# Last mixture by expert regions in DRAM, layer 0's head sums all on PE, other landing costs and another stage order

## The chip, the cores and the metric

The kernel runs as one program on one core of a Trainium2 chip. Its time is the device time of one execution in microseconds. Six resources matter here: PE (TensorE, matmuls and transposes), DVE (VectorE), ACT (ScalarE), POOL (GpSimd), SP (SyncE, which only issues transfers) and the 16 DMA engines that carry all transfers, whichever engine issued them. Each engine executes its own instructions strictly in program order. An instruction that waits for a semaphore holds up everything behind it on that engine, and nothing on the others.

## The reference, cut to what matters

Input `x` is 16 batches of 256 tokens of 128 numbers, and there is a context of 64 keys per batch. Four layers follow one another, and each has an attention to the context and a feed-forward part, added to `x` with a gate.

```python
x = x + tanh(g_xattn[0]) * L0_attention(layernorm(x), ctx)   # softmax over the 16 heads
x = x + tanh(g_ffn[0])   * L0_ffn(layernorm(x))              # 8 experts, top 2, and a shared expert
x = x + tanh(g_xattn[1]) * L1_attention(layernorm(x), ctx, bias, mask)
x = x + tanh(g_ffn[1])   * L1_ffn(layernorm(x))              # ternary weight
x = x + tanh(g_xattn[2]) * L2_attention(layernorm(x), ctx, mask)
x = x + tanh(g_ffn[2])   * L2_ffn(layernorm(x))              # one expert in effect
x = x + tanh(g_xattn[3]) * L3_attention(layernorm(x), ctx, masks)
x = x + tanh(g_ffn[3])   * L3_ffn(layernorm(x))              # 8 experts, the best one
```

Two parts are touched. In layer 0 the attention's softmax runs over the heads, not over the keys:

```python
energy = einsum('bhqd,bhkd->bhqk', Qh, Kh) * scale
attn = softmax(energy, axis=1)                   # axis 1 is the 16 heads
out = einsum('bhqk,bhkd->bhqd', attn, Vh)
```

The last feed-forward part sends each token to the one expert with the largest probability:

```python
logits = t @ switch_w + switch_b
route_prob = softmax(logits, axis=-1)
route_prob_max = max(route_prob, axis=-1)
routes = argmax(route_prob, axis=-1)
for e in range(8):
    y = gelu(t @ w1[e] + b1[e]) @ w2[e] + b2[e]
    out = where((routes == e)[:, None], y, out)
out = out * route_prob_max[:, None]
```

## The kernel before

All of `x` stays in SBUF, one tile `xs[b]` per batch. The work is written as some hundreds of generators ("tasks"): for example `unit0(pair, t)` is layer 0's attention for two batches and half of their queries, `attention(l, b)` is that of one batch in layers 1 to 3, and `sorted_pair(l, hf, q)` is two expert tiles. The batches form two halves, `hf` 0 and 1, of eight batches or 2048 tokens, and every mixture of experts works by half. Two batches form a block (`blk`).

**What sets the order.** A planner, the class `Order`, runs the tasks when the program is built. Each task states its next step as an engine, an estimated length and the things it needs, or as a transfer with a size, or as a buffer that it wants. The planner always takes the step that can begin first by its own estimate, and among equals the one of the lowest rank (`RANKS`, one number per half and stage; stages 0 and 1 are layer 0's attention and mixture, 7 is the last mixture). Its order is then the written order of each engine; POOL is chained in the same order. A transfer is taken to land `LAND` us after its issue plus its size over `RATE`, and an indirect gather 2.2 us after its issue. These numbers decide only the order. The chip's semaphores decide when things run.

**Layer 0's attention** (`unit0`, L816 to L927): scores on PE (L833), their largest over the heads on DVE (L844, L849), differences (L852), exponentials on ACT (L865), sums over the 16 heads, reciprocals, products on POOL (L894), values on PE (L910). The sums have two forms. For the first half, 16 matmuls with the identity add up the heads in a PSUM bank (L871), and DVE takes the reciprocal from it (L877). For the second half, POOL adds eight heads to eight (L883), and DVE adds up the rest (L886) and takes the reciprocal (L889). The buffer of L883 comes from the same four `big` buffers that hold the experts' hidden values.

**Layer 0's mixture** (`mixture` with `l` = 0): each block is normalized and its rows stored to DRAM (`keep`); when all four blocks of the half have their logits, one chain of DVE steps finds the experts and every token's place in an order sorted by expert, padded to tiles of 128 rows. A matmul with a one-hot matrix (L1528 to L1549) turns that into a list, for every row of every tile, of the token that belongs there. There are 39 tiles in each half. For every tile, SP reads the tile's expert number into a register and fetches this expert's packed weights (578 KB, L1647, six buffers), POOL gathers the tile's rows by an indirect transfer (L1671), PE transposes them (L1684) and multiplies by the first weights (L1698), ACT applies the gelu (L1705, or its tanh form in layer 3), PE multiplies by the second weights (L1717), and DVE adds the bias (L1727). The results are stored and later gathered back per token (`collect`, L1779, L1787).

**The last mixture** (`mixture` with `l` = 3) does the same with one expert per token, 23 tiles per half. Its DRAM rows hold the normalized row and `x` itself (`keep` and `keep_x`, issued by SP). The one-hot list also carries the token's gate, in three bfloat16 parts. The tile's result, times the gate, plus `x` (L1734), goes straight to its rows of the output by an indirect scatter on POOL (L1753). POOL so issues 124 gathers of rows (78 for layer 0, 46 here), 64 gathers of `collect` and 46 scatters.

Other lines that are named below: L644 and L647 to L650 belong to the layernorm (DVE, then POOL), L669 and L747 to the queries, L972 prepares layer 1's attention bias, loaded by SP four transfers a batch into one of three buffers, L1093 takes the scores' largest in layers 2 and 3, and L1392 adds the router's bias.

## Time and profile before

| | |
|---|---|
| Median of 3 runs | 1087.75 us (1085.69 to 1087.98) |
| The profiled execution, reported time | 1091.78 us |
| The profiled execution, span of its instructions | 1090.0 us |
| Granted PE clock, mean over the span | 0.927 |
| DMA bytes | 114.36 MB, 105 GB/s over the span |

| Stage in the profiled execution | from, us | to, us |
|---|---|---|
| Layer 0's attention, first half (`unit0`) | 20.6 | 110.4 |
| Layer 0's attention, second half | 106.8 | 281.5 |
| Layer 0's expert tiles, first half | 171.4 | 342.9 |
| Layer 0's expert tiles, second half | 337.1 | 516.7 |
| Layer 1's attention, both halves | 419.1 | 769.0 |
| Layer 2's attention, both halves | 551.0 | 887.1 |
| Layer 3's attention, both halves | 649.3 | 963.6 |
| Last mixture's routing, first half | 798.7 | 851.2 |
| Last mixture's expert tiles, first half | 855.6 | 1072.9 |
| Last mixture's routing, second half | 971.5 | 994.2 |
| Last mixture's expert tiles, second half | 984.2 | 1087.2 |

The second table is made from the trace: each instruction of DVE, ACT and POOL was put to its task by its place in the engine's order, and the first start and the last end of each task's instructions were taken. The end of the first half's last tiles (1072.9) is that of their scatters on POOL.

In the profile's lines, `x` and a number is a count of instructions, and "busy" is the time in which an engine executed an instruction. Matmul records overlap, as matmuls are pipelined: 16 records of L1698 in a row pass in 1.79 us though each lasts some 300 ns. A 128-wide matmul in float32 leaves two records. In a table by stretches of time, each engine's busy time is followed by its number of instructions, and then come the granted PE clock (1 is full speed), the mean busy share of the DMA engines and the bytes moved per second. In the chain of waits, each line is a start, a length and the work, and "issue" is time in which the engine waited for nothing that the profile shows. In a group's line, the busy time, the mean of one in ns, and the idle time before the group with what ended most of it stand at the right.

### The profile page before, as it was taken

The page shows a single profiled execution, that of the slowest core. Times are in us where ns is not written, and L with a number is a line of the kernel's source. Part 1 is how long each engine was busy: PE and PEld are TensorE (multiplying, and loading weights), DVE is VectorE, ACT ScalarE, POOL GpSimd, SP SyncE. Part 2 cuts the span into 40 slices and gives each one's busy share as a digit, 9 for nine tenths or more (in the row PEclk, how much of TensorE's full clock was granted, in tenths as well). Part 3 has the DMA queues.
Part 4 walks back from the last instruction along what each step waited for, and adds up shares of the span by engine and source line. Part 5 has one row for each costly group of instructions (what it writes and reads, how often), then busy time and mean ns, then how long its engine had stood idle before and what let it go on. Part 6 is the DMA issues. An engine that isn't in the chain of part 4 may idle for free.

```text
span 1090.0 us, 27621 instructions
## 1 busy us (share of the span) xinstructions
PE 914.4 (84%) x10480; PEld 724.2 (66%) x10480; DVE 670.9 (62%) x1832; ACT 575.9 (53%) x1345; POOL 644.8 (59%) x1055
## 2 busy tenths in 40 slices
PE   5887568989788987789789899999998999777765
PEld 3776346878686886677556667667665667666664
DVE  4798897754464224366776767879789645446221
ACT  5454243656443454566446557765765667553332
POOL 5787636666834654765557656533444666744675
PEclk9899788979889998899999999999999999987987
DMA  6000004467764774633100100100000425544672
GB/s 195 2 12 21 23 1 147 132 211 237 231 153 162 227 228 141 228 93 112 52 17 20 29 16 21 36 21 7 24 9 2 161 59 156 189 145 144 215 259 60
DMA packets 63477, 114.36 MB, mean 105 GB/s; under 512 B 10289, under 2 KB 42552, under 8 KB 63344
## 3 DMA queue, kind: packets, MB, share of 16 engines
q1 hardware_dynamic: 54688, 94.22, 26.8%
q0 software_dynamic: 8224, 17.45, 6.0%
q8 instruction: 82, 1.34, 0.5%
q10 hardware_dynamic: 432, 0.93, 0.3%
q14 instruction: 51, 0.42, 0.1%
HBM read 99.06 MB, written 14.42 MB: 104 GB/s over the span
## 4 chain that ended last, share of the span: by engine, by line
PE 38%; DVE 12%; issue 8%; DMA 6%; POOL 5%; ACT 3%; another core or an unknown queue 2%; SPq 0%; POOLq 0%; DVEq 0%; ACTq 0%
PE bank L1698 6%; PE bank L1717 6%; DMA xg<-xrow,state 4%; DVE mx L1093 3%; PE bank L1008 3%; PE bank L1175 3%; PE bank L1072 2%; PE bank L781 2%; PE bank L1134 2%; PE bank L1014 2%; PE bank L747 1%; PE bank L1197 1%; PE bank L669 1%; PE bank L1621 1%
## 5 line engine op out<-in xcount | busy, mean ns | idle before, releaser
L1705 ACT ACTIVATE big<-bank,wb 128x128 f32<-128x128 f32 x496 | 138.5, 382 | 156.2 <-issue 98.6
L1698 PE MATMUL bank<-xgT,wb 128*128 128x128 f32 x992 | 147.5, 301 | 21.9 <-DVE xgT L1688 14.0
L1671 POOL DMA_INDIRECT xg<-xrow,state x124 | 121.9, 983 | 63.5 <-issue 27.9
L1698 PEld LDWEIGHTS bank<-xgT,wb 128*128 128x128 f32 x992 | 134.1, 212 | 31.7 <-DVE xgT L1688 18.6
L1717 PE MATMUL bank<-wb,big 128*128 128x128 f32 x992 | 133.6, 287 | 5.8 <-issue 4.8
L1717 PEld LDWEIGHTS bank<-wb,big 128*128 128x128 f32 x992 | 126.2, 200 | 13.8 <-issue 10.9
L656 ACT ACTIVATE xn<-x,ln 128x128 f32<-128x128 f32 x256 | 107.6, 494 | 52.5 <-POOL ln L650 52.2
L1727 DVE TENSOR_TENSOR y<-bank,wb 128x128 f32<-128x128 f32 x124 | 32.3, 285 | 115.4 <-PE bank L1717 90.9
L894 POOL TENSOR_TENSOR pT<-pT,rc 128x1024 f32<-128x1024 f32 x32 | 75.2, 2366 | 45.2 <-DVE rc L889 12.3
L1779 POOL DMA_INDIRECT yg<-ysort,state x64 | 62.9, 983 | 56.5 <-DVE x L1787 26.3
L1093 DVE TENSOR_REDUCE mx<-bank 128x8 f32<-128x512 f32 x128 | 81.4, 682 | 20.9 <-PE bank L1014 6.3
L1162 ACT ACTIVATE pT<-bank 128x512 f32<-128x512 f32 x128 | 67.2, 601 | 36.3 <-PE bank L1149 30.2
L677 POOL TENSOR_TENSOR x<-x,rows_sb 128x256 f32<-128x256 f32 x96 | 71.3, 761 | 12.5 <-ACT xn L656 11.8
L644 DVE BATCH_NORM_STATS2 ln<-x 128x6 f32<-128x128 f32 x256 | 68.6, 268 | 2.4 <-DMA x<-in_x_dram 2.2
L648 POOL TENSOR_TENSOR ln<-ln,mhalf 128x4 f32<-128x4 f32 x64 | 66.7, 1043 | 5.3
L1008 PE MATMUL bank<-kexp,qT 32*128 32x256 f32 x768 | 69.4, 413 | 0.2 <-DVE mx L1093 0.2
L647 POOL TENSOR_SCALAR ln<-ln 128x4 f32<-128x4 f32 x64 | 14.7, 230 | 90.9 <-DVE ln L645 83.7
L1753 POOL DMA_INDIRECT out_dram<-y,state x46 | 47.1, 1023 | 27.6 <-DVE y L1727 20.6
L1046 DVE TENSOR_REDUCE mx<-bank 128x8 f32<-128x512 f32 x64 | 43.5, 682 | 29.8 <-PE bank L1014 14.2
L1175 PE MATMUL bank<-pT,vx 128*32 128x256 f32 x768 | 60.3, 399 | 0.8 <-DVE pT L1054 0.5
L1688 DVE COPY xgT<-bank 128x256 f32<-128x256 f32 x64 | 25.9, 409 | 55.1 <-PE bank L1684 37.9
L1684 PE MATMUL bank<-ident,xg 128*128 128x128 f32 x124 | 29.4, 306 | 34.2 <-DMA xg<-xrow,state 30.1
(230 smaller groups left out, 2094.2 us busy)
## 6 DMA issues: line engine op xcount, KB each, us to landing
wb<-in_pk_l_dram SPq DMA_DIRECT2D x124, 578.0 KB
ysort<-y SPq DMA_DIRECT2D x38, 128.0 KB
xrow<-xn SPq DMA_DIRECT2D x16, 256.0 KB
fill<-in_fsideT_dram SPq DMA_DIRECT2D x64, 64.0 KB
x<-in_x_dram SPq DMA_DIRECT2D x16, 128.0 KB
xrow<-x SPq DMA_DIRECT2D x16, 128.0 KB
xg<-xrow,state POOLq DMA_INDIRECT x124
yg<-ysort,state POOLq DMA_INDIRECT x64
```

The source lines that it names most:

```text
L644: nc.vector.bn_stats(st[:, 2 * i + j, :], xs[b][:, j, :])
L656: nc.scalar.activation(xn[:, k, :], xs[b][:, j, :], AF.Identity, bias=nm[:, k : k + 1], scale=rs[:, k : k + 1],)
L677: nc.gpsimd.tensor_tensor(xs[b], xs[b], row.unsqueeze(1).to_broadcast([P, 2, D]), ALU.add)
L894: nc.gpsimd.tensor_tensor(s3, s3, rc.ap.unsqueeze(1).to_broadcast([P, 8, P]), ALU.mult)
L1008: nc.tensor.matmul(dst(g), qT[strip(g), ts], kexp[strip(g)].rearrange("p h k -> p (h k)"), start=True, stop=False,)
L1093: nc.vector.tensor_reduce(mx[:, :, g, :], sc[g].ap.rearrange("p (t h k) -> p t h k", h=4, k=S2), AX.X, ALU.max,)
L1162: nc.scalar.activation(pTs[g // 2].ap[:, (g % 2) * 512 : (g % 2 + 1) * 512], sc[g].ap, AF.Exp)
L1175: nc.tensor.matmul(po.ap[strip(g), i * S : (i + 1) * S], vx.ap[:, b % 2, c, :], pTs[c // 4].ap[:, (c % 4) * S : (c % 4 + 1) * S], start=Tr ...
L1671: nc.gpsimd.indirect_dma_start(out=xg[i], out_offset=None, in_=xd, in_offset=bass.IndirectOffsetOnAxis(ap=index[:, 2 * q + i : 2 * q + i + ...
L1698: nc.tensor.matmul(ph.ap[:, cs], wb[i].ap[:, cs], xgT.ap[:, i * P : (i + 1) * P], start=True, stop=True,)
L1705: nc.scalar.activation(hb.ap[:, i, cs], ph.ap[:, cs], func, bias=wb[i].ap[:, PK_B1 + c : PK_B1 + c + 1],)
L1717: nc.tensor.matmul(py.ap[:, i * D : (i + 1) * D], hb.ap[:, i, c * P : (c + 1) * P], wb[i].ap[:, PK_W2 + c * D : PK_W2 + (c + 1) * D], star ...
```

## The change

Four things change.

1. **The last mixture works by expert regions.** `mixture` is split into `first_mixture` (layer 0, otherwise as before) and `last_mixture`. In DRAM every expert has a region of 2048 rows and a gap of 128, so 17280 rows per half, each of 258 numbers: the normalized row, `x`, the token's number and its gate. A running count per expert (`next_`) gives every token its row as soon as its own block's experts are known, so each block makes its own routing (30 DVE instructions in place of 9, and in place of most of the chain of 47 per half), and POOL scatters its four times 128 rows into the regions. Every tile is then 128 rows that lie one after another. SP reads the tile's first row into a register and loads them by a plain transfer. No one-hot list is made. A closing chain of 13 DVE instructions per half gives each tile's expert, first row and number of filled rows. Rows that no token fills must hold finite numbers, so `fill_regions` first writes all rows with 54 transfers of 660 kB on SP from one constant tile. Two small DVE instructions per tile give empty rows a place beyond the output, where the scatter drops them.
2. **Layer 0's sums** over the heads are made by PE in both halves.
3. **The planner's numbers:** an indirect gather of layer 0 is taken to land 3.2 us after its issue rather than 2.2, and `RATE` is 280 kB/us rather than 250.
4. **Other ranks**, so another order of the stages.

The instruction streams as built show the following. PE: of the last mixture's 46 tiles, seven are finished before the last attention matmul, where it was twelve. POOL issues 220 indirect transfers rather than 234. SP issues 382 transfers rather than 306. ACT loads its tables 26 times rather than 36.

```diff
-REACH, LAND, RATE, SWAP = 0.1, 1.8, 250e3, 1.3
+REACH, LAND, RATE, SWAP = 0.1, 1.8, 280e3, 1.3
...
-RANKS = ((11, 14, 2, 14, 3, 5, 4, 14), (14, 14, 4, 14, 6, 9, 6, 2))
+RANKS = ((0, 14, 14, 14, 1, 15, 10, 14), (14, 14, 4, 8, 9, 12, 13, 15))
...
+ROW3 = 2 * D + 2
+REGION = NT * P
+NROWS = E * REGION + (E - 1) * P
...
-        if pair < HB // 2:
-            (pb,) = yield get(banks, 1)
-            at = yield op(PE, 3.6, at, pb)
-            for h in range(H):
...
-        else:
-            (sb,) = yield get(big_s, 1)
-            sm = sb.ap.rearrange("p a b -> p (a b)")
-            at = yield op(POOL, 2.4, at, sb)
-            nc.gpsimd.tensor_tensor(sm, ss[0].ap, ss[1].ap, ALU.add)
-            (rc,) = yield get(rc0_s, 1)
-            at = yield op(DVE, 2.85, at, rc)
-            nc.vector.tensor_reduce(
-                rc.ap, sm.rearrange("p (h q) -> p q h", q=P), AX.X, ALU.add
-            )
-            nc.vector.reciprocal(rc.ap, rc.ap)
-            give(sb, big_s, at)
+        (pb,) = yield get(banks, 1)
+        at = yield op(PE, 3.6, at, pb)
+        for h in range(H):
+            nc.tensor.matmul(
+                pb.ap[:, 0:P], ident, ss[h // 8].ap[:, (h % 8) * P : (h % 8 + 1) * P],
+                start=(h == 0), stop=(h == H - 1),
+            )
+        (rc,) = yield get(rc0_s, 1)
+        at = yield op(DVE, 0.95, at, rc)
+        nc.vector.reciprocal(rc.ap, pb.ap[:, 0:P])
+        give(pb, banks, at)
...
+    def last_mixture(hf, rank, begin):
...
+        def block(blk):
...
+            (xn,) = yield get(big_s, 1, begin[bs[0]], begin[bs[1]])
+            rows = xn.ap.rearrange("p (t c) -> p t c", c=ROW3)
+            ats = yield from layernorm(blk, begin, rows[:, :, 0:D], xn)
...
+            for i, b in enumerate(bs):
+                yield op(ACT, 0.35, begin[b])
+                nc.scalar.copy(rows[:, 2 * i : 2 * i + 2, D : 2 * D], xs[b])
...
+            nc.tensor.matmul(pb.ap[:, 0:32], ones, cnt, start=True, stop=True)
+            nc.tensor.matmul(pb.ap[:, 32:64], before, cnt, start=True, stop=True)
...
+            nc.vector.tensor_copy(acc3[:, :, 0], next_)
+            nc.vector.tensor_copy(acc3[:, :, 1:5], et(pb.ap[:, 0:32]))
+            nc.vector.tensor_tensor_scan(
+                upto, carry4.rearrange("p e t -> p (e t)"), acc, 0.0, ALU.mult, ALU.add
+            )
+            nc.vector.tensor_copy(next_, upto3[:, :, 4])
...
+            for t in range(t0, t0 + 4):
+                at = yield op(POOL, 1.3, placed)
+                part_indirect()
+                ins = nc.gpsimd.indirect_dma_start(
+                    out=xd,
+                    out_offset=bass.IndirectOffsetOnAxis(ap=pos[:, t : t + 1], axis=0),
+                    in_=rows[:, t - t0, :],
+                    in_offset=None,
+                )
...
+    def fill_regions(hf, whens):
+        xd = srt[3, hf][2].rearrange("(p a) c -> p a c", p=P)
+        n, m = NROWS // P, 5
+        for i in range(n // m):
+            yield dma(SP, 4.0 * P * m * ROW3, whens[i * m * len(whens) // n])
+            nc.sync.dma_start(
+                xd[:, m * i : m * (i + 1), :],
+                rows_sb[:, 0:ROW3].unsqueeze(1).to_broadcast([P, m, ROW3]),
+            )
...
         for i in range(m):
+            if l == 3:
+                yield op(SP, 0.4, *xgs, *needs)
+                r = nc.sync.value_load(
+                    ex.ap[0:1, n + 2 * q + i : n + 2 * q + i + 1], min_val=0, max_val=NROWS - P
+                )
+                at = yield dma(SP, 132e3)
+                nc.sync.dma_start(xg[i], xd[bass.ds(r, P), :])
+                done_with(ex, at)
+                continue
             at = yield op(POOL, 1.3, *xgs, *needs)
...
-        at = (at[0] + 2.2, "DMA")
+        if l == 0:
+            at = (at[0] + 3.2, "DMA")
...
+                nc.vector.tensor_tensor(
+                    place[:, i : i + 1], xg[i][:, 2 * D : 2 * D + 1].bitcast(I32),
+                    filled[:, t : t + 1], ALU.bitwise_and,
+                )
+                nc.vector.tensor_tensor(
+                    place[:, i : i + 1], place[:, i : i + 1], empty[:, t : t + 1], ALU.bitwise_or
+                )
...
+    whens = [X[i][b] for i, h in ((5, 0), (6, 0), (3, 1), (4, 1)) for b in range(HB * h, HB * h + HB)]
+    for hf in range(2):
+        order.task(100.0, fill_regions(hf, whens[16 * hf : 16 * hf + 16]))
```

`whens` is a need of the planner alone: it says after which steps a fill may be placed, and no semaphore stands for it.

## The prediction, made before the result was known

> **What bounds the kernel now.** I first read the page's busy shares, then the same by stretches of time, then the chain of waits from the last instruction, then the groups of instructions.
>
> ```profile
> span 1090.0 us, 27621 instructions
> PE 914.4 (84%) x10480; PEld 724.2 (66%) x10480; DVE 670.9 (62%) x1832; ACT 575.9 (53%) x1345; POOL 644.8 (59%) x1055
> ...
> q1 hardware_dynamic: 54688, 94.22, 26.8%
> ```
>
> No engine fills the span, and 84% on PE is an average of unlike stretches. From the tiles' names I cut at 517 (the last layer 0 expert tile) and 964 (the last attention matmul), and subdivided.
>
> ```profile
> core 0: us, PE busy (x) PEld busy (x) DVE busy (x) ACT busy (x) POOL busy (x), PEclk, DMA share, GB/s
> 0.00:171.00 171.00, 122.00 (x1884) 95.41 (x1885) 138.70 (x313) 74.76 (x140) 108.54 (x145) 0.87 0.14 41
> 171.00:342.00 171.00, 151.84 (x1647) 129.03 (x1646) 99.13 (x245) 94.86 (x236) 106.16 (x117) 0.90 0.60 187
> 342.00:517.00 175.00, 147.93 (x1281) 128.74 (x1285) 70.86 (x205) 90.73 (x238) 105.84 (x170) 0.93 0.56 175
> 517.00:675.00 158.00, 141.15 (x1738) 98.11 (x1731) 116.72 (x329) 89.40 (x190) 94.86 (x186) 0.98 0.09 25
> 675.00:855.00 180.00, 172.01 (x2280) 123.33 (x2278) 150.30 (x440) 114.43 (x249) 83.14 (x189) 0.99 0.07 20
> 855.00:964.00 109.00, 97.40 (x1090) 73.96 (x1091) 52.65 (x161) 72.02 (x163) 69.33 (x123) 0.97 0.43 136
> 964.00:1090.00 126.00, 82.11 (x575) 75.57 (x573) 42.53 (x145) 39.73 (x134) 76.94 (x127) 0.85 0.56 177
> 1016.00:1090.00 74.00, 48.22 (x338) 44.79 (x338) 16.31 (x52) 21.06 (x76) 46.83 (x77) 0.85 0.54 169
> ```
>
> To 171 VectorE is fullest (139 of 171). From 171 to 517 PE leads and transfers are heavy. From 517 to 855 PE and VectorE are dense and transfers nearly absent. From 855 to 964 VectorE falls to half and PE from 96% to 89%: one half's layer 3 attention runs beside the other half's first expert tiles. The last 126 us finish 34 of the 46 expert tiles, 3.7 us each, with every engine idle a third of the time or more. The chain there says why:
>
> ```profile
> 984.36 11.31 issue
> ...
> 997.31 6.65 DMA xg<-xrow,state
> ...
> 1007.57 8.37 DMA xg<-xrow,state
> ...
> 1030.76 1.02 POOL out_dram L1753
> 1032.17 1.00 POOL out_dram L1753
> 1033.58 1.00 POOL out_dram L1753
> 1034.97 4.84 DMA xg<-xrow,state
> ...
> 1063.50 4.67 DMA xg<-xrow,state
> ```
>
> Gathers sit on POOL behind the result's scatters, 1.4 us apart; PE waits for them with nothing else left.
>
> **The change, part by part**, as three stretches of the profiled execution (span 1090.0, reported 1091.8; the median shown is 1087.75, so 2.2 us come off a sum of spans).
>
> ```profile
> L871 PE MATMUL bank<-pT,ident 128*128 128x128 f32 x256 | 36.0, 309 | 9.9 <-DVE pT L852 4.4 <-DVE vx L807 3.0 <-ACT pT L865 2.5
> L883 POOL TENSOR_TENSOR big<-pT,pT 128x1024 f32<-128x1024 f32 x8 | 18.9, 2360 | 20.9 <-PE bank L1607 17.9 <-ACT pT L865 3.0
> L886 DVE TENSOR_REDUCE rc<-big 128x128 f32<-128x1024 f32 x8 | 15.3, 1912 | 2.8 <-POOL big L883 2.8
> L1671 POOL DMA_INDIRECT xg<-xrow,state x124 | 121.9, 983 | 63.5 <-issue 27.9 <-PE bank L1607 27.6 <-PE bank L1717 2.9
> ```
>
> *Layer 0, to 517.* Eight units of the second half lose L883 and L886 (18.9 us of POOL, 15.3 of VectorE) and gain the first half's form: 36.0 us of PE busy, 4.5 each; the reciprocal stays. In the built order three of the eight sums stand ahead of the first routing, where PE idles 49 of 171 us: free. Five stand behind it, where PE is busy 152 of 171: 5 x 4.5 = 22.5 us added. Against that, the five no longer put 5 x 2.36 = 12 us ahead of gathers in POOL's queue (L883 once waited 17.9 us for its buffer, and everything on POOL with it), and ScalarE's table loads up to here fall from 25 to 19 in the built order, 6 x 1.28 = 8 us. I take two thirds of these 20 back: +8. Bounds: +22.5 with nothing given back, and 22.5 - 20 - 10 = -8 if VectorE's relief (5 x 1.9) counts too. The later landing (3.2 for 2.2) and the faster rate are numbers of the planner: no instruction, only order. POOL's new constants, some 2 us of memsets and iotas, fall before 60 us.
>
> *Attention, 517 to 964: 447 us.* In the built order seven expert tiles, not twelve, are finished by PE ahead of the last attention matmul, and both halves go through layers 1 to 3 closer together. So the thin part (855 to 964) should resemble the dense one. VectorE is the measure: 319.7 us busy now. Off: the first routing of layer 3 (47 instructions, 18.2), five tiles at 0.85 (4.3). On: 21 small instructions more per block, at 0.19 (L1392's 179 ns for 128x32), for six blocks 24; the closing 13 instructions 5; two per tile for seven tiles 2. That makes 328. At a VectorE share of 0.78, between the first and second dense stretch (0.74 and 0.835), 421 us: -26. Bounds: 393 at 0.835, 459 at today's whole-stretch 0.715: -54 to +12. I take the middle of the dense rows, since the work mix is theirs.
>
> Also here: 54 region fills (each 660 kB, 35.7 MB) on SP. The q1 row gives 94.22 MB in 26.8% of 1090 us, 322 GB/s, so 111 us of wire where 7 to 9% is used. They precede bias loads (L972's) by two to eight fills, at most 8 x 2.05 = 16 us of delay; those loads are issued three batches ahead, so I charge nothing. Uncovered, the four runs (2, 4, 3, 8) cost 17 x 2.05 = 35. The other 37 fills stand on SP between the last bias load and layer 3's first weight fetch, 76 us against the hundred or more that layer 2's and 3's attention of the first half still takes there. Two waits are new. A half's first region scatter waits for its 27 fills, and with it all of POOL, layernorm included; the first read of the regions waits on SP for all 16 scatters, with every later weight fetch behind it. The first is hidden by the same hundred us, the second by the six weight buffers already filled; if either cover went, the price is what is left of the 76, or one scatter's way (1.4 to issue, 4.7 to 8.4 to land in the chain's rows). The region scatters add 32 on POOL while 46 gathers leave; 24 row stores leave SP; ScalarE's 16 copies of x, 0.4 each, have slack (114 of 180 busy).
>
> *Tail: 126 us.* Of the tiles, 39 now end behind the last attention matmul. Each moves 592 + 132 + 66 = 790 kB, 2.45 us at 322 GB/s. PE needs 16 passes at 112 ns each (the chain has 16 in 1.79) and two transposes, about 2.1, or 2.5 at the clock of 0.85. SP issues two register-loaded transfers a tile, at 1.2 apart (its issues at 1009.49 and 1010.66) 2.3. POOL keeps one scatter, 1.4. VectorE 1.2. So the floor is 96 us, and the ceiling the 3.5 us a tile of 1016 to 1090 (21 tiles in 74), 137. I take 2.8, nearer the floor because the waits in the chain were for gathers that POOL issued late, and 8 us to drain: 117, so -9. Bounds -22 to +19. The second half's routing (971 to 994, a gap in PE before) now has 16 tiles of the first half to hide it.
>
> The built order puts each pair's two gathers on SP behind that pair's two weight loads; POOL had its own queue. The Trainium skill, "DMA: Bandwidth & Descriptors", Queues, rings and completion order, says each engine consumes a ring's descriptors in order, which speaks against this move: an uncovered gather would come 3.7 us later by 2 x 592 kB at 322 GB/s, 20 pairs 74 us, and the sum would be 1135. No row of before shows it, as no gather was on SP. I keep to the sum, because three pairs of buffers are in flight.
>
> Sum: 517 + 8 + 447 - 26 + 126 - 9 = 1063, less 2.2: **1061**.
>
> **Rivals.** *A, PE becomes layer 0's bound:* the five sums behind the routing cost their 22.5 and nothing comes back, +22.5 for +8: 1076. For: PE is 89% busy from 171 to 342. Against: POOL's and ScalarE's waits there.
> *B, the tail is transfer-bound at the rate it has (ends slower):* 39 x 0.79 MB at 177 GB/s is 174 us, with 8 drain 182, not 117: 1126. For: the most bytes are packed into the end. Against: single stretches of 10 us hold 329 GB/s at DMA share 0.98, so 177 is no limit of the wire. It decides at 144 us: over 3.5 a tile, under 226 GB/s.
> *C, the new order doesn't tighten the attention:* VectorE's share stays 0.715, because PE's fixed order waits on chains (layernorm, routing, bias loads) in new places: 459 for 421, 1099. For: moved priorities guarantee no density, and each block gains a serial chain of some 25 small VectorE steps. Against: 338 us at 0.79 exist already.
>
> **How the numbers follow.** Forecast 0.50 (its own range 1044 to 1074), A 0.17, B 0.13, C 0.20. 0.2% is 2.2 us, about what a measurement can tell. Faster: 0.49 + 0.15 + 0.02 + 0.04 = 0.70; same 0.04; slower 0.26, mostly B and C. The range goes from 1040 (attention and tail both halfway to their better bounds, 14 and 7 less) to 1100, just past C and short of B.
>
> **What would show it.** Right: layer 0's last expert tile near 525; last attention matmul near 946 with VectorE at 0.78 from there back; a tail of 117 us, above 250 GB/s, with no POOL scatter ahead of a gather in the chain. Wrong: PE waiting for bias loads between 525 and 750 (fills), the SP queue waiting on gathers in the tail, or tiles at over 3.5 us; or layer 0 past 540, with PE's sums on the chain.

## The result, and the profile after

| | time |
|---|---|
| before, median of 20 runs | 1090.58 us (1085.69 to 1098.28) |
| after, median of 20 runs | 1083.24 us (1072.46 to 1095.38) |
| ratio, with its 95% interval | 0.9901 (0.9878 to 0.9925) |

The change makes the kernel 1.0% faster, 7 to 11 us. The forecast was 27: the sign was right, and less than half of the size came. The kernel before took 1090 us in two of the six sets of runs below and 1036 to 1039 in the other four, for a cause that stays open, so times are compared by their ratio to the kernel before in the same set, and stages only between sets of one such level. The same cuts as in the prediction (layer 0's last expert tile, the last attention matmul, the end) give:

| stretch | before | forecast | after | difference, forecast | difference, measured |
|---|---|---|---|---|---|
| layer 0 | 517 | 525 | 526.7 | +8 | +10 |
| attention | 447 | 421 | 430.7 | -26 | -16 |
| tail | 126 | 117 | 124 | -9 | -2 |
| span | 1090.0 | 1063 | 1081.1 | -27 | -9 |

The first lines of the page of the kernel after, and its DMA queue:

```profile
span 1081.1 us, 28618 instructions
PE 932.2 (86%) x10728; PEld 745.6 (69%) x10728; DVE 675.9 (63%) x2019; ACT 569.4 (53%) x1357; POOL 610.1 (56%) x1030
...
q1 hardware_dynamic: 88160, 131.77, 42.0%
```

PE works 18 us more than before (932 for 914) in a span that is 9 us shorter, so its idle time fell by 27. VectorE, which the forecast followed, works 5 us more. The kernel after by the three stretches (the same columns as in the prediction):

```profile
0.00:171.00 171.00, 131.39 (x2016) 103.61 (x2016) 138.25 (x318) 70.23 (x135) 102.19 (x149) 0.88 0.15 43
171.00:526.70 355.70, 314.83 (x3033) 271.91 (x3032) 158.39 (x443) 184.21 (x479) 201.04 (x292) 0.94 0.57 175
526.70:957.40 430.70, 396.17 (x5030) 284.74 (x5031) 326.25 (x1010) 264.84 (x582) 247.29 (x492) 0.99 0.48 123
957.40:1081.10 123.70, 89.78 (x656) 85.37 (x654) 53.05 (x252) 50.08 (x163) 59.62 (x98) 0.86 0.69 224
```

The kernel before by the same three stretches, in rows that the prediction had only in pieces:

```profile
171.00:517.00 346.00, 299.77 (x2928) 257.77 (x2931) 169.99 (x450) 185.59 (x474) 212.00 (x286) 0.92 0.58 181
517.00:964.00 447.00, 410.56 (x5107) 295.41 (x5100) 319.66 (x928) 275.86 (x600) 247.33 (x497) 0.98 0.16 50
```

Take PE's busy time from each length. In the attention PE idled 36.4 us before (447.0 less 410.6) and idles 34.5 after (430.7 less 396.2). By this account the stretch is 16 us shorter because 14 us of PE's busy time have left it, and not because it became denser. Most of that work is not gone: five expert tiles that were finished ahead of the last attention matmul are now finished behind it. PE's transposes and multiplications of expert tiles take 32.0 us of the attention before and 20.2 after, and PE would be busy for 383.9 and 378.9 us without them: by these two counts the tiles make 9 to 12 of the 14. In the tail PE's work grew from 82.1 to 89.8 and its idle time fell from 43.9 to 33.9. To layer 0's last tile its work grew by 24.5 and its idle time fell from 95.2 to 80.5.

The chain of waits of the kernel after, at the place where the first half's tiles end and the second half's begin:

```profile
1007.88 0.30 DVE y L1899
...
1009.33 0.31 SPq L1809
...
1011.01 5.50 DMA xg<-xrow
...
1018.00 2.08 PE bank L1868 x8
...
1020.50 3.38 PE bank L1868 x16
1023.88 1.79 PE bank L1889 x16
```

L1899 is a tile's addition of the bias on VectorE, L1809 a fetch of weights on SP, `xg<-xrow` a tile's rows coming from a region, L1868 and L1889 the two multiplications (eight records a tile each). Further down, L1854 is the transposes of a tile's rows on PE, L1858 the copy of what they give (`xgT`) out of PSUM, and L1640 a matmul of the routing, which waits for VectorE's steps (`rt`). A tile's time below is the start of its L1899 in the trace. The first half's last tile is put out from 1007.9 on. The second half's first pair follows at 1014.7, and the second pair ends its multiplications at 1025.7 and is put out by 1026.9: some 19 us for four tiles, where the other 19 of the second half take 47, 2.5 each. So about 9 us are lost between the halves. The rows for that pair came at 1016.5, after a stretch in which SP, issuing in order, had been busy with weights. PE's clock in stretches of 5 us tells of a second loss there:

```profile
1010.00:1015.00 5.00, 4.79 (x29) 4.55 (x27) 0.28 (x1) 2.28 (x8) 1.23 (x3) 0.66 0.93 295
1015.00:1020.00 5.00, 2.48 (x10) 2.18 (x11) 1.81 (x9) 0.00 (x0) 2.42 (x4) 0.69 0.93 296
1020.00:1025.00 5.00, 5.00 (x31) 5.00 (x30) 0.42 (x1) 3.31 (x12) 0.00 (x0) 0.63 0.29 105
1025.00:1030.00 5.00, 4.76 (x42) 4.57 (x42) 2.02 (x9) 2.14 (x9) 2.41 (x4) 1.00 0.57 184
```

After a gap the granted clock is 0.63 to 0.69, and 16 matmuls take 3.38 us instead of 1.79. PE then counts as busy while it works at less than its pace.

The first half's last tiles, ahead of this place, are slow too: from 957.4 to 1007.9 PE finishes 16 of them in 50.5 us, 3.2 each, at a clock of 0.83, and waits 5.1 us at two strokes for the second half's routing (in the lines of waits: PE's line, what it waited for, us in total, times, longest):

```profile
957.40:1007.90 50.50, 38.57 (x267) 36.74 (x265) 28.61 (x145) 24.53 (x71) 28.86 (x48) 0.83 0.73 234
```

```profile
PE bank L1640 <- DVE rt L1320: 3.1, 1, 3.1
PE bank L1640 <- DVE rt L1319: 2.0, 1, 2.0
```

### The profile page after: what moved, and what is told of

Same layout as the page of the kernel before. It is cut to its first block, busy times and chain, and to the rows that moved or that the text cites. A ratio compares the mean times of both kernels' runs of the same rounds, so it can differ in the third digit from the quotient of the medians.

```text
span 1081.1 us, 28618 instructions
## 1 busy us (share of the span) xinstructions
PE 932.2 (86%) x10728; PEld 745.6 (69%) x10728; DVE 675.9 (63%) x2019; ACT 569.4 (53%) x1357; POOL 610.1 (56%) x1030
## 4 chain that ended last, share of the span: by engine, by line
PE 54%; DVE 23%; issue 7%; POOL 6%; DMA 4%; ACT 4%; another core or an unknown queue 1%; SPq 0%; POOLq 0%; DVEq 0%; ACTq 0%
PE bank L1868 9%; PE bank L1889 8%; PE bank L1187 4%; PE bank L1020 4%; PE bank L895 3%; PE bank L1748 2%; PE bank L1762 2%; DVE mx L1105 2%; PE bank L1146 2%; PE bank L1026 2%; PE bank L1084 2%; DVE ov L869 2%; DVE pT L877 2%; PE bank L806 2%; DVE ln L669 1%
## 5 line engine op out<-in xcount | busy, mean ns | idle before, releaser
L1868 PE MATMUL bank<-xgT,wb 128*128 128x128 f32 x992 | 140.6, 293 | 26.5 <-DVE xgT L1858 13.5
L1868 PEld LDWEIGHTS bank<-xgT,wb 128*128 128x128 f32 x992 | 129.8, 206 | 34.5 <-DVE xgT L1858 16.8
L1889 PE MATMUL bank<-wb,big 128*128 128x128 f32 x992 | 134.3, 288 | 4.3 <-ACT big L1875 2.0
L1889 PEld LDWEIGHTS bank<-wb,big 128*128 128x128 f32 x992 | 126.8, 202 | 8.9 <-ACT big L1875 4.7
L681 ACT ACTIVATE xn<-x,ln 128x128 f32<-128x128 f32 x224 | 94.0, 493 | 48.8 <-POOL ln L675 48.8
L1899 DVE TENSOR_TENSOR y<-bank,wb 128x128 f32<-128x128 f32 x124 | 32.6, 288 | 132.0 <-PE bank L1889 87.1
L1840 POOL DMA_INDIRECT xg<-xrow,state x78 | 76.0, 974 | 48.4 <-DVE state L1540 18.5
L1105 DVE TENSOR_REDUCE mx<-bank 128x8 f32<-128x512 f32 x128 | 81.0, 682 | 13.1 <-PE bank L1026 9.4
L672 POOL TENSOR_SCALAR ln<-ln 128x4 f32<-128x4 f32 x64 | 14.7, 230 | 129.3 <-DVE ln L670 121.8
L1174 ACT ACTIVATE pT<-bank 128x512 f32<-128x512 f32 x128 | 67.2, 604 | 34.0 <-PE bank L1161 30.6
L1934 POOL DMA_INDIRECT out_dram<-y x46 | 46.3, 1006 | 56.5 <-DVE y L1899 49.7
L702 POOL TENSOR_TENSOR x<-x,rows_sb 128x256 f32<-128x256 f32 x96 | 68.7, 734 | 16.0 <-ACT xn L681 15.3
L895 PE MATMUL bank<-pT,ident 128*128 128x128 f32 x512 | 69.1, 300 | 9.8 <-DVE pT L877 4.4
L895 PEld LDWEIGHTS bank<-pT,ident 128*128 128x128 f32 x512 | 67.3, 215 | 12.8 <-ACT xn L681 4.6
L1090 ACT ACTIVATE pT<-bank 128x512 f32<-128x512 f32 x64 | 37.0, 604 | 43.7 <-PE bank L1084 32.5
```

What stands on the lines that cost most here:

```text
L681: nc.scalar.activation(xn[:, k, :], xs[b][:, j, :], AF.Identity, bias=nm[:, k : k + 1], scale=rs[:, k : k + 1],)
L702: nc.gpsimd.tensor_tensor(xs[b], xs[b], row.unsqueeze(1).to_broadcast([P, 2, D]), ALU.add)
L895: nc.tensor.matmul(pb.ap[:, 0:P], ident, ss[h // 8].ap[:, (h % 8) * P : (h % 8 + 1) * P], start=(h == 0), stop=(h == H - 1),)
L1105: nc.vector.tensor_reduce(mx[:, :, g, :], sc[g].ap.rearrange("p (t h k) -> p t h k", h=4, k=S2), AX.X, ALU.max,)
L1840: nc.gpsimd.indirect_dma_start(out=xg[i], out_offset=None, in_=xd, in_offset=bass.IndirectOffsetOnAxis(ap=index[:, 2 * q + i : 2 * q + i + ...
L1868: nc.tensor.matmul(ph.ap[:, cs], wb[i].ap[:, cs], xgT.ap[:, i * P : (i + 1) * P], start=True, stop=True,)
```

## The experiments

Each is an edit of the kernel after unless it says otherwise. "Ratio" is always to the kernel before in the same set, with its 95% interval.

### The two kernels again, and the parts one by one

> The kernel before, for its stages on the same chip as the runs beside it. If PE sets the attention stretch, PE's idle time between layer 0's last expert tile and the last attention matmul is the same as in the changed kernel within 4 us (36 and 35 in the profiles at hand: 447 less 411 busy, 431 less 396). If VectorE's share sets it, the changed kernel idles less there by 10 or more.

> The changed kernel, for its stages and its ratio on the same chip as the runs beside it: 0.988 to 0.993 of the time before, layer 0 later by 5 to 12 us than in the kernel before, the attention stretch shorter by 13 to 20 and the tail by 0 to 6.

PE's idle time and the three stretches came out as expected. The ratio did not: the kernel after has 0.9947 (0.9914 to 0.9981) in this set, above the 0.988 to 0.993 that were expected. Layer 0's last tile, the last attention matmul and the end stand at 521.7, 970.1 and 1094.8 before, and at 532.8, 966.6 and 1090.7 after: +11 for layer 0, -15 for the attention, -1 for the tail. PE's idle time in the attention is 35.3 and 34.1 us. So the first reading above is no accident of one profile. A third run of the kernel after, in a later set, is below.

**Layer 0's sums alone**, in the kernel before:

```diff
-        if pair < HB // 2:
-            (pb,) = yield get(banks, 1)
...
-        else:
-            (sb,) = yield get(big_s, 1)
...
+        (pb,) = yield get(banks, 1)
+        at = yield op(PE, 3.6, at, pb)
+        for h in range(H):
+            nc.tensor.matmul(
```

> The kernel before with layer 0's sums of the second half on PE, nothing else. Theory 'the sums cost as forecast': layer 0's last tile comes 5 to 12 us later than in the kernel before and the time is 1.005 to 1.011 of it. Rival 'they cost nothing, since PE's added work fills idle time and POOL and VectorE are relieved': within 0.3% of the time before, or faster.

Measured: 1.0378 (1.0336 to 1.0420), some 40 us slower, where the forecast had 8 for this part. Three rows of the kernel before in this set, and three of this kernel:

```profile
171.00:521.70 350.70, 301.76 (x2920) 260.20 (x2922) 166.44 (x452) 185.24 (x473) 212.17 (x287) 0.91 0.57 179
521.70:970.10 448.40, 413.06 (x5116) 297.90 (x5110) 319.22 (x927) 275.95 (x600) 247.18 (x497) 0.98 0.16 50
970.10:1094.80 124.70, 82.49 (x578) 75.87 (x576) 42.73 (x147) 40.04 (x135) 76.74 (x127) 0.84 0.56 179
```

```profile
171.00:540.70 369.70, 320.27 (x3068) 278.99 (x3070) 166.54 (x448) 180.92 (x475) 203.24 (x289) 0.93 0.54 169
540.70:1001.80 461.10, 425.91 (x5119) 307.61 (x5112) 314.93 (x924) 276.17 (x613) 261.57 (x512) 0.98 0.18 56
1001.80:1124.60 122.80, 67.98 (x478) 62.59 (x476) 38.63 (x131) 34.45 (x112) 66.86 (x110) 0.82 0.49 156
```

Layer 0 is 19 us longer, near the 22.5 of rival A. The attention is 13 us longer too, although nothing in it was edited: PE works 425.9 us there instead of 413.1, with the same idle time (35.2), because the planner now places more tiles ahead of the last attention matmul: 18 are put out by then instead of 12. In the tail stand 100 fewer matmul records, and yet it is only 2 us shorter. So one edit in layer 0 moves the written order of everything behind it.

**Layer 0's sums undone**, in the kernel after: the `else` branch above comes back.

> The changed kernel with layer 0's sums of the second half back on POOL and VectorE. Theory 'the sums cost as forecast': layer 0's last expert tile, at 526.7 in the changed kernel, comes some 8 to 10 us earlier, and the time is 1074 or so. Rival 'the sums were free, and the other order made layer 0 longer': the last tile stays at 525 or comes later by up to 10, because gathers and products stand behind POOL's additions again, and the time is 1083 to 1093.

Measured: 0.9877 (0.9837 to 0.9917), no slower and no surely faster than the change. The last tile of layer 0 is at 488.3. The rival holds: the kernel after, in its third run (a set of the same level), has it at 486.2, so undoing the sums does not bring layer 0's end forward. The planner's order moves here too: the attention is 409.5 us for 419.6 and the tail 125.8 for 117.2. With the new ranks the sums on PE cost nothing that can be measured, nor do they gain anything.

**The old ranks** in the kernel after:

```diff
-RANKS = ((0, 14, 14, 14, 1, 15, 10, 14), (14, 14, 4, 8, 9, 12, 13, 15))
+RANKS = ((11, 14, 2, 14, 3, 5, 4, 14), (14, 14, 4, 14, 6, 9, 6, 2))
```

> The changed kernel with the ranks of the kernel before. Theory 'PE sets the attention stretch, so where tiles stand moves the time only through PE's idle time': more tiles stand ahead of the last attention matmul, the stretch is longer by what the tail is shorter, and the time is within 6 us of the changed kernel's. Rival 'the new ranks carry the gain': 10 us slower or more, not faster than the kernel before.

Measured: 1.0601 (1.0562 to 1.0641). Beside 0.9947 in the same set this is 72 us, by far the largest effect of any line of the change. The attention and the tail of this kernel, and its longest wait of PE from 1047 on:

```profile
548.90:1047.60 498.70, 434.91 (x5095) 312.02 (x5095) 333.45 (x1085) 286.55 (x637) 273.61 (x525) 0.95 0.49 125
1047.60:1156.00 108.40, 57.96 (x407) 53.64 (x407) 33.45 (x155) 29.90 (x101) 34.45 (x57) 0.75 0.51 169
```

```profile
PE bank L1854 <- DMA xg<-xrow: 25.0, 3, 17.6
```

PE idles 64 us in this attention instead of 34 and works 35 more in it, as it now finishes all 23 tiles of the first half there. The added idle time has no single cause: PE's longest waits are 16.5 us in 12 pieces for a step of VectorE in each attention (L1218; 8.4 in the kernel after) and 9.0 at one stroke for a layernorm's output on ScalarE. The first half's last tile is put out from 1003.5 on, ahead of the last attention matmul at 1047.6, so nothing is left to cover the second half's routing: PE waits 17.6 us at one stroke for the second half's first rows. This is the cover that the prediction named for the tail, and this is its price when it is gone, but it is not the whole loss: layer 0 is 16 us longer, the attention idles 30 more, and the tail, with 16 tiles fewer in it, is only 16 shorter.

**The regions alone**, in the kernel before: the kernel after with the old sums, the old numbers of the planner and the old ranks.

> The kernel before with the expert regions and nothing else: the old sums, planner's numbers and ranks. Theory 'the regions are worth 1.8%, whatever the order' (the changed kernel against the one without regions): 0.978 to 0.988 of the time before. Rival 'the order decides, since the old ranks were chosen for another routing': over 1.01.

Measured: 1.0363 (1.0309 to 1.0417). The rival holds. This kernel shows the same hole, to the tenth of a microsecond (L1867 are its transposes):

```profile
PE bank L1867 <- DMA xg<-xrow: 26.4, 5, 17.6
```

**All but the regions**: the kernel before with PE's sums, the new numbers and the new ranks.

> The kernel before with the sums all on PE, the new landing time and rate, and the new ranks: all of the change but the expert regions. Theory 'the regions bring what gain there is': it is 1.003 to 1.010 of the time before, as PE's added 25 us in layer 0 are not paid back. Rival 'the new order brings the gain': 0.995 or less.

Measured: 1.0091 (1.0056 to 1.0126), as the first theory had it. In another set of the same level the kernel after had 0.9912 (0.9876 to 0.9948). The quotient is 0.982: in the new order the regions are worth some 18 us. Where they lie is plain from the attention and the tail without regions, and then with them (the third run of the kernel after):

```profile
486.50:904.60 418.10, 391.21 (x5011) 281.16 (x5012) 313.86 (x908) 259.00 (x559) 237.40 (x478) 0.99 0.14 42
904.60:1040.10 135.50, 92.36 (x684) 86.64 (x682) 46.25 (x158) 47.17 (x161) 92.78 (x149) 0.88 0.64 202
```

```profile
486.20:905.80 419.60, 392.76 (x5018) 283.44 (x5019) 323.75 (x1010) 264.41 (x580) 246.23 (x490) 0.98 0.51 126
905.80:1023.00 117.20, 85.25 (x668) 81.01 (x666) 53.01 (x252) 50.85 (x166) 61.01 (x101) 0.92 0.73 238
```

Layer 0 ends at 486.5 and 486.2, the attention lasts 418 and 420, the tail 135.5 and 117.2. All of it is tail. PE's waits in the two tails say what went, first without regions (there the transposes are L1671, the first multiplication L1685 and the copy L1675), then with:

```profile
PE bank L1671 <- DMA xg<-xrow,state: 22.1, 10, 4.2
PE bank L1685 <- DVE xgT L1675: 13.5, 12, 2.1
```

```profile
PE bank L1868 <- DVE xgT L1858: 14.7, 10, 3.4
PE bank L1854 <- DMA xg<-xrow: 4.4, 5, 3.4
```

The waits for gathered rows fall from 22.1 us to 4.4, and the difference is nearly the whole gain. The waits for the copies stay.

### What sets the attention

The prediction measured the attention by VectorE's share. Four edits of the kernel after change the work of one engine and leave every instruction in its place.

```diff
-                nc.vector.tensor_reduce(
+                for r in range(1 + (g == 1)):
+                    nc.vector.tensor_reduce(
```

> The changed kernel with one of the four reductions of the scores' largest done twice in each of the 32 attentions of layers 2 and 3: 32 x 0.68 = 22 us more on VectorE, in the same order, nothing else. Theory 'VectorE's share measures the attention' (the prediction's step): the stretch from layer 0's last tile to the last attention matmul grows by 22 or more (22 / 0.757 = 29). Rival 'PE sets it, VectorE has slack': it grows by 0 to 8.

```diff
-                for g in range(4):
+                for r in range(4 * i, 8):
+                    g = r % 4
                     nc.tensor.matmul(
                         dst(g),
...
-                        start=True, stop=False,
+                        start=True, stop=(r < 4),
```

> The changed kernel with a quarter... half of the first pass of score matmuls done twice in the same 32 attentions: 128 matmuls more, 32 x 0.78 = 25 us of PE by the group's 50.0 us for 256, in the same order, nothing else. Theory 'PE sets the attention': the stretch grows by 20 to 26. Rival 'VectorE's share measures it': it grows by under 8, as PE would fill idle time.

```diff
-                    mx[:, :, g, :], sc[g].ap.rearrange("p (t h k) -> p t h k", h=4, k=S2),
+                    mx[:, :, g, :], sc[g].ap.rearrange("p (t h k) -> p t h k", h=4, k=S2)[:, :, :, 32:64],
```

> The changed kernel with the reduction of the scores' largest in layers 2 and 3 done over 32 of the 64 keys: 128 instructions of VectorE that take about 0.36 us instead of 0.68, 41 us less, in the same order, nothing else. Theory 'VectorE sets the attention': the stretch falls by 35 or more. Rival 'PE sets it': by 0 to 8. Rival 'the two by turns, each attention being a chain through both': by 12 to 30.

```diff
-                for h in range(2):
+                for h in range(0):
                     for g in range(4):
                         nc.tensor.matmul(
                             dst(g),
                             ks[strip(g), h].rearrange("p h e k -> p (h e k)"),
```

> The changed kernel without the 512 matmuls that add the mask's fill in the second pass of layers 2 and 3 (31.9 us of PE in the profile after, both groups together), in the same order; this part of the mask is left out of the computation. Theory 'PE sets the attention': the stretch falls by 26 or more. Rival 'VectorE sets it': by 0 to 8. Rival 'by turns': by 10 to 25.

They are set against the third run of the kernel after:

> The changed kernel, for its stages on the same chip as the three beside it: 0.988 to 0.995 of the time before.

Measured: 0.9912 (0.9876 to 0.9948), as expected. The attention rows of the four, in the order of the edits; that of the kernel after is shown above:

```profile
485.50:922.80 437.30, 401.44 (x5019) 286.34 (x5020) 344.71 (x1042) 264.05 (x580) 246.25 (x490) 0.98 0.52 121
```

```profile
492.50:920.10 427.60, 401.54 (x5275) 294.17 (x5275) 325.27 (x1010) 265.11 (x580) 246.34 (x490) 1.00 0.53 124
```

```profile
490.70:900.90 410.20, 386.39 (x5019) 280.02 (x5020) 295.21 (x1010) 264.23 (x580) 247.06 (x489) 1.00 0.52 129
```

```profile
483.00:897.80 414.80, 384.84 (x4506) 271.56 (x4507) 323.79 (x1010) 264.14 (x580) 246.87 (x489) 0.97 0.51 127
```

| edit | busy time of the engine, us | the stretch, us | us of the stretch per us of the engine | ratio of the whole |
|---|---|---|---|---|
| none | | 419.6 | | 0.9912 (0.9876 to 0.9948) |
| more on VectorE | +21.0 | +17.7 | 0.84 | 1.0107 (1.0063 to 1.0150) |
| less on VectorE | -28.5 | -9.4 | 0.33 | 0.9813 (0.9757 to 0.9868) |
| more on PE | +8.8 | +8.0 | 0.91 | 0.9984 (0.9951 to 1.0017) |
| less on PE | -7.9 | -4.8 | 0.61 | 0.9880 (0.9821 to 0.9939) |

Neither theory of a single engine holds. Work that is added is paid almost in full on either engine. Work that is taken away comes back by a third on VectorE and, as far as one profile tells, by somewhat more on PE. The ratio of the last row cannot be told from no change. That fits two engines that take turns in a fixed order, each attention being a chain through both, but it is not shown: the two removals also fell short of what was expected for turns (9.4 for 12 to 30, 4.8 for 10 to 25). The edits on PE were smaller than their expectations priced them, because a group's records overlap those of other groups: the 128 added matmuls cost 13.5 us of their group's busy time and 8.8 of the stretch's, and the 512 that are left out have 31.9 and 7.9.

The prices are rough for another reason. PE's busy time is no fixed amount of work: with some 5019 matmul records each, it is 401.4 us with more on VectorE, 392.8 in the kernel after and 386.4 with less on VectorE, and the granted clock of these stretches goes from 0.97 to 1.00. What part of this the edits caused was not separated.

**The fills.** The 54 transfers that write the regions first were moved from 527-761 to the first 200 us:

```diff
-    whens = [X[i][b] for i, h in ((5, 0), (6, 0), (3, 1), (4, 1)) for b in range(HB * h, HB * h + HB)]
+    whens = [(45.0 + 4.0 * i, "DMA") for i in range(32)]
```

> The 54 region fills are placed in the first 170 us, where the DMA engines are nearly idle (a share of 0.14 before), instead of 527 to 761, where the changed kernel's trace shows the DMA share at 0.54 to 0.61 and single stretches of 10 us full. Theory 'the fills cost': bias loads and weight fetches are held behind them, so the stretch from layer 0's last tile to the last attention matmul (430.7 us in the changed kernel) loses 5 to 12 us and the whole time with it, to some 1073. Rival 'the attention is held by PE itself' (its share there is 0.91 to 0.95 already): the stretch stays within 3 us and so does the time; what the fills now do to the first 170 us (input loads beside them) may cost up to 3.

Measured: 0.9922 (0.9892 to 0.9951), no change, and the attention lasts 413.0 with transfers nearly gone from it:

```profile
488.20:901.20 413.00, 389.44 (x5005) 277.30 (x5006) 324.14 (x1020) 266.73 (x582) 247.55 (x499) 0.99 0.10 32
```

The 413.0 stand beside 419.6 of the kernel after, but two of its expert tiles are put out in them instead of six, at 2.4 us of PE each. So the fills cost nothing that can be measured in the attention, as the prediction charged them. Its price of the wire was too low. In the changed kernel 37 fills and eight bias loads (26 MB) take 640 to 750 at a full queue:

```profile
q1 hardware_dynamic: 25937, 26.00, 101.2%
```

That is 236 GB/s, not the 322 that weight loads had: 54 fills are some 150 us of wire rather than 111.

### What sets the tail

**The routing first.** The blocks' routing of the last mixture gets a better rank than its tiles:

```diff
-            order.task(rank, block(blk))
+            order.task(rank - 4, block(blk))
```

> The blocks' routing of the last mixture gets a rank four better than the tiles, so that the second half's rows should be scattered before the first half's last tiles. Theory 'the handover costs': the gap between the first half's last tile and the second half's first (1007.9 to 1014.7 and 1025.7, where 2.4 us a tile would be the pace) closes, worth 6 to 10 us: 1073 to 1077. Rival 'the routing is late because the attention ahead of it is late': the last attention matmul moves later by about what the gap loses, and the time stays within 3 us of 1083.

Measured: 1.0110 (1.0077 to 1.0143). Neither theory holds. The last attention matmul is at 925.8, some 20 us later than in the kernel after at the same level, and the tail is no shorter (125.8). The gap did not close either, although the rows came early: the second half's last scatter into the regions starts 32 us ahead of the first half's last tile instead of 9, and from that tile to the second half's second pair it is 17.2 us, as in the kernel after (17.1). So it is not the routing that holds the rows between the halves.

**The copies to ScalarE.**

```diff
-        at = yield op(DVE, 0.17 * m, at, xgT)
-        nc.vector.tensor_copy(xgT.ap[:, 0 : m * P], pt.ap[:, 0 : m * P])
+        if l == 3:
+            at = yield op(ACT, 0.4, at, xgT)
+            nc.scalar.copy(xgT.ap[:, 0 : m * P], pt.ap[:, 0 : m * P])
+        else:
+            at = yield op(DVE, 0.17 * m, at, xgT)
+            nc.vector.tensor_copy(xgT.ap[:, 0 : m * P], pt.ap[:, 0 : m * P])
```

> In layer 3's expert tiles the copy of the transposed rows out of PSUM goes to ScalarE instead of VectorE. Theory 'the tail's tiles are paced by VectorE's order' (PE waits 2.0 to 2.6 us a pair between the transposes and the first multiplication, while the copy stands behind the pair before's output steps): the tail of 123.7 us falls by 10 to 20 and the time to 1065 to 1075. Rival 'the tail is paced by transfers' (224 GB/s there): the tail changes by less than 4 us, and PE's waits go to the rows' loads instead.

Measured: 0.9794 (0.9762 to 0.9827), the best kernel of this study, 1.1 to 1.5% faster than the change by its three ratios. Its tail puts out 42 tiles, where that of the kernel after puts out 40, and lasts 113.3 instead of 117.2:

```profile
898.10:1011.40 113.30, 89.11 (x702) 82.20 (x700) 47.61 (x238) 58.81 (x192) 66.16 (x108) 0.97 0.78 262
```

This looked like the proof of the theory. Two more kernels say that it isn't. With the old sums as well:

> The changed kernel with layer 0's sums of the second half back on POOL and VectorE, and with layer 3's copies of the transposed rows on ScalarE. If the two add: 0.968 to 0.978 of the time before, the tail near 113 as with the copies alone. If the planner's other order eats one of them: 0.980 to 0.990.

Measured: 0.9932 (0.9898 to 0.9967), a tail of 124.2, and 13.6 us of PE waiting for rows. And with the copies on ScalarE, but the planner told that they are on VectorE, so that all else stays in the changed kernel's order:

> The changed kernel with layer 3's copies of the transposed rows on ScalarE, with every other instruction in the changed kernel's own order. Theory 'the copies behind VectorE's output steps pace the tail': the tail loses 6 to 12 us (20 pairs at 0.3 to 0.6) and the time is 0.980 to 0.986 of the time before. Rival 'the earlier gain came from the planner's other order': 0.989 to 0.994, as the changed kernel.

Measured: 0.9888 (0.9837 to 0.9940). The ratio lies beside the rival's range and cannot be told from that of the kernel after, but its interval reaches into the theory's range too. The tail decides for the rival: it is 115.8 us for 117.2, where the theory asked for 6 to 12 less. PE's longest waits in this tail, to be read beside the pair of lines shown above for the kernel after (L1872 is the first multiplication here, L1859 the copy):

```profile
PE bank L1854 <- DMA xg<-xrow: 10.2, 11, 4.0
PE bank L1872 <- ACT xgT L1859: 5.8, 11, 0.9
```

The wait for the copies fell from 14.7 to 5.8 us and the wait for rows rose from 4.4 to 10.2. Once the second half's tiles run, the transfers are nearly full, as these 15 us show, of the kernel after (third run) and then of this one:

```profile
985.00:1000.00 15.00, 12.98 (x115) 12.73 (x114) 6.19 (x27) 7.73 (x30) 6.17 (x11) 1.00 0.94 311
```

```profile
985.00:1000.00 15.00, 14.04 (x121) 13.42 (x120) 5.01 (x24) 9.31 (x35) 6.51 (x13) 1.00 0.96 330
```

A DMA share of 0.94 leaves little room for faster copies: the second half's last 19 tiles take 44.1 us instead of 46.2. And what the copies gave there was lost between the halves, where 6.4 of the 10.2 us of waiting for rows lie (3.4 of 4.4 in the kernel after): from the first half's last tile to the last of the second pair it takes 21.0 us instead of 17.9. So the first of the three kernels has its gain from its order, in which the second half's first tile comes 8 us after the first half's last and the second pair 5 us later; with the copies moved and the order held these are 8 and 12.

**The rows off SP's queue.** The rows of the regions are loaded by ScalarE's queue instead of SP's, at the same places:

```diff
-                r = nc.sync.value_load(
+                r = nc.scalar.value_load(
...
-                nc.sync.dma_start(xg[i], xd[bass.ds(r, P), :])
+                nc.scalar.dma_start(xg[i], xd[bass.ds(r, P), :])
```

> The changed kernel with the plain loads of the last mixture's rows issued by ScalarE instead of SP, at the same places of the order, so that they no longer stand behind weight loads. Theory 'SP's order holds them': the handover (first tile of the second half after the last of the first, some 7 us, and the next pair 11 us later) shrinks by 4 to 8 and the tail with it. Rival 'the rows wait for the region scatters and for buffers, whichever engine issues them': the tail stays within 3 us, or grows by up to 6 as ScalarE's gelus stand behind the loads' waits.

Measured: 1.0020 (0.9992 to 1.0047), 11 us slower than the change. The tail is 119.9 for 117.2, and from the first half's last tile to the second half's second pair it takes 16.7 us for 17.1. The attention is 8 us longer; in 4.1 us of them PE waits at one stroke for a layernorm's output on ScalarE, and the rest was not traced. What holds the rows between the halves is not SP's queue alone.

## Why the prediction was half right

**Layer 0, +8.** Measured +10 and +11 in the sets at 1090 us: the size was right there. The reason given, five sums at 4.5 us less two thirds of what POOL and ScalarE give back, is not shown by it. Undoing the sums at the other level did not move layer 0's end, and doing them alone in the old order cost 19 us there and 40 in all. So the agreement may be luck. Rival A's price is thus real in one order and absent in another.

**The attention, -26; measured -16.** This is the step that failed most: "VectorE is the measure", 328 us of work at a share of 0.78. The work was foreseen (326), the share was 0.757. What the step left out is that PE was busy for 411 of 447 us before. At PE's 396 us of remaining work, 421 would have asked PE to idle 25 us where it idled 36, and nothing in the change did that at this level (at the other one the kernel after idles 27; the kernel before has no profile there). The four edits show that a microsecond less on VectorE is worth a third of one. By PE's account the stretch became shorter for another reason than the forecast's, PE's 14 us, mostly the five tiles that moved behind it; no run held the rest and moved the tiles alone. The prediction counted those tiles only by their 4.3 us of VectorE work, and their PE time is in the tail now.

**The fills at nothing.** Right in the sum.

**The tail, -9; measured -2.** The mechanism was right: waits for rows went, 17.7 us of them in the comparison without regions. The rate of a running second half, 2.5 us a tile, is even the "floor" of 2.45. The term that was too small is the 2.8 us for the first half's tiles. The 16 of them take 50.5 us, where 2.8 each make 44.8, and these 6 us are nearly all of the difference between 117 and 124. "The second half's routing now has 16 tiles of the first half to hide it", but PE, in its fixed order, waits 5.1 us for that routing among them, and its clock is 0.83. The second half's 23 tiles take 65.6 us from the first half's last tile on, where 2.8 each make 64.4: the 9 us that are lost between the halves are paid for by the 2.5 us of the tiles behind. In the third run, at the other level, the 16 tiles take 45.5 us at a clock of 0.92, and the tail is 117.2. What sets the moment of the second pair's rows is left open: neither another queue for them nor an earlier routing brought it forward. Rival B, a tail bound by 177 GB/s, fell: the tail moves 224 GB/s, and some 300 where it runs freely.

**The rows behind the weights on SP.** The prediction weighed 1135 us for rows that come late there. It did not come so: PE waits 2.2 us for rows in the whole tail of the kernel after, and with the rows on another queue nothing is gained. That three pairs of buffers covered it, as the sum had assumed, fits this and was not tested.

**Rival C** was priced as 38 us on the attention when the new order does not tighten it. VectorE's share rose from 0.715 to 0.757, two thirds of the way that the forecast asked for, while PE's stayed (0.918 and 0.920), and the kernel is faster all the same. But orders that are bad by that amount and more exist next door: the old ranks cost 65 us in the attention of the changed kernel. The prediction gave the ranks no term of their own; it read the built order's tile counts and took the stages for additive. The parts aren't: sums alone +3.8%, regions alone +3.6%, everything but the regions +0.9%, and all together -1.0%. That the regions pay with the new ranks and not with the old ones is shown by these runs; the sums pay with neither (0.9877 without them, 0.9912 with them in the new order), and no run has the new ranks alone. Why the planner's order with the old ranks leaves PE idle 64 us in the attention was not traced beyond the two waits named above.

## What to carry to other kernels

Where one engine is busy for nearly the whole of a stretch (here 411 of 447 us), the shares of the others say little of what it can lose: write "length = busy + idle" for the fullest engine, before and after, and ask which of the two the change touches. Take the busy part with care, as it moved by 6 to 9 us here with the same instructions. Where a planner fixes the order, an edit's own price (here 1 to 2%) can be smaller than what its new order does (4 to 7%), and an effect seen in one order must be tried again with every instruction held in its place before it is called a cause. A wait that is taken away can turn up as another one further on, as that for the copies did between the halves.

## What the runs showed of the hardware that was not expected

- **The PE clock after a gap.** With the old ranks, PE worked for 0.09 us between 1060 and 1065 and not at all for the next ten; the granted clock is 0.50 from 1050 to 1085 in stretches of 5 us, though PE is busy for 4.48 us of the last of them, and 1.00 from 1090. The Trainium skill, "TensorE: Matmul & The Clock Gate", What's actually happening, says that the throttled state is the default and that activity releases it; these rows agree, and they say what a hole costs beyond its length, as the 3.38 us above do.
- **The wire's rate by transfer.** Region fills ran at 236 GB/s with the queue full, while the second half's tiles reached 311 to 330 GB/s at a share of 0.94 to 0.96. One thing that differs is the packets: the 26.00 MB of the fills' stretch came in 25937 packets, 1.0 KB each, where the 94.22 MB of the whole kernel before came in 54688, 1.7 KB each. Whether that makes the rate was not tested.
